# Last-use pools, earlier fetches and a kept-clear last chain in a two-layer graph kernel

## The chip, the core and the metric

The kernel runs as one program on one core of a Trainium2 chip. A core has five engines with a queue of instructions each, worked off strictly in order: PE (matrix products into eight banks of PSUM), DVE and ACT (elementwise work), POOL (here it only issues gathers) and SP (here it only issues transfers). Engines wait for each other and for transfers through semaphores; whatever stands behind a waiting instruction in its queue waits too. The metric is the device time of one execution in microseconds (us), the median of several runs.

## The reference

Two rounds of a graph network over 6250 nodes and 100000 edges, then a residual and a layer norm:

```python
def _gin_agg(h, src, dst, eps, n_nodes):
    agg = jax.ops.segment_sum(h[src], dst, num_segments=n_nodes)
    return (1.0 + eps) * h + agg

h = _gin_agg(x, src, dst, eps1, n)            # width 256
h = relu(h @ W1a + b1a)
h = relu(h @ W1b + b1b)                       # width 512; the kernel calls it h1
h = _gin_agg(h, src, dst, eps2, n)            # width 512
h = relu(h @ W2a + b2a)
out = h @ W2b + b2b                           # width 256
x = _layernorm(x + out, axis=-1)
```

The edges are sorted by `dst`, and `dst` is the square of a uniform number, so low nodes receive most of the edges.

## The kernel before, in words

Nodes are held in 49 tiles of 128 rows (tile 48 has 106). Edges are held in 782 chunks of 128. The kernel works in two layers, one after the other, and each layer sums messages in two ways.

*Heavy tiles (0 to 6)* receive so many edges that their sums are a dense product: a table of counts (how many edges run from each source to each node) times the rows. In layer 1 the counts are built on the core ("counting"), used (L1606) and also stored in DRAM (`counts`). In layer 2 they come back as `ci`, are converted by ACT into `cf` (L1399), and multiply the rows of h1, which are fetched as `xr` for a *range* of four tiles at a time and split by ACT and DVE into an upper and a lower half (L1362, L1363, L1367). There are 13 ranges; range 12 holds tile 48 alone, range 11 tiles 44 to 47. The products of one range with one heavy tile are eight matmuls, upper and lower half in turn (L1470, `second_products`). `AHEAD2` ranges, from the highest down, are already worked in layer 1, once counting is over.

*All other edges* are gathered: POOL issues one indirect DMA per chunk (L488), 494 in each layer, into two rings (`early`, and in layer 2 also `late`). The rings hold six pieces of four chunks. PE adds up a piece with a one-hot matrix `sel` (L1066), ACT copies the sum out of PSUM (`split`, L1100 or L1108), PE puts the parts of a group of chunks in their places (L1119, with `to`), and DVE adds them to the tiles' accumulators (L1129). Groups are worked from the highest nodes down to the lowest.

When a tile has all its sums, its *dense* part follows: PE transposes the accumulator (L1165), ACT copies it (`zt`, L1177), PE multiplies by the first weights (L1204), ACT applies bias and relu (`ht`, L1214), PE multiplies by the second weights (L1233). Then DVE and ACT finish h1 (`h1r`, L1243 and L1245) and ACT stores it (L1246) in layer 1; in layer 2 residual and norm follow, and SP stores the output. An accumulator is seeded: SP fetches the tile's own rows, and ACT scales them by 1 + eps (L916).

The last group of layer 1 reaches tiles 6 and 7. So layer 2 begins with a group (`FORE`, 12 chunks) that gathers only from rows which do not include tiles 6 and 7 (`h1[: GAP + 1]`); what comes from these two is counted and added separately (`late_edges`, `adding_late`). All later gathers of layer 2 may touch any row of h1, so they wait until tiles 6 and 7 are stored.

The order of instructions on every engine is written by a planner, `Plan`, while the program is built. It plays the kernel through with costs that stand in the code (`LOAD = 6.0`, `COUNTS = 12.0`, `SEEDS = (6.0, 12.0)`, `PASS`, `act()`, `dve()`), and each step asks for an engine with a priority (a smaller number goes first). The planner is run for each layer apart. It decides orders alone; when something runs is left to the semaphores.

On-chip memory comes from stacked pools. Those of layer 1 are closed before those of layer 2 are opened in the same place, so a tile of layer 2 waits until the tile that lay there in layer 1 has been used for the last time:

```python
for name in ("first", "keep1", "loan1")        # layer 1
for name in ("keep2", "loan2")                 # layer 2
acc_room = Tiles(keep if once else loan, [P, TILES, width], F32, "acc", ACCS if once else ACCS2)
```

`first` holds layer 1's weights, `keep1` everything from `sel` to `h1r` and the accumulators. The pool `wide2` on the other side, for the second products, is opened when counting is over.

Of the kernel before, what the change touches and what calls it, by code (L numbers as in the profile page):

```python
# [10 lines left out]
F32 = mybir.dt.float32  # L11
# [35 lines left out]
PASS = 0.00042  # L47
LATE = (6, 8)
HASTE = -14.0
AHEAD2 = 1  # L50
ACCS2 = 4
AFTER = 4.0
# [300 lines left out]
def tile_gin_residual_layernorm(  # L353
# [105 lines left out]
    FORE = next(g for g in range(BEGIN[1], NG) if lo[g] >= max(HEAVY[1], LATE[0]))  # L459
    orders = {1: list(reversed(range(BEGIN[0], NG)))}  # L460
    orders[2] = [FORE] + [g for g in reversed(range(BEGIN[1], NG)) if g != FORE]
# [7 lines left out]
    FORE0, FOREN = groups[FORE][0], len(members[FORE])  # L469
# [7 lines left out]
    def gather(number, i, table, width, *places):  # L477
# [7 lines left out]
        if number == 2 and pieces[number][i][0] == FORE:  # L485
            table, rows_in, first = h1[: GAP + 1, :], fore, FORE0
# [281 lines left out]
    def ordered(ctx):  # L768
# [17 lines left out]

        def layer(number, pools, table, width, scale, weights, ba, wide, at=None, aside=None, right=None):
# [5 lines left out]
            keep, loan, last_ = pools  # L793
# [14 lines left out]
            def reach(g):  # L808

                return range(lo[g] if once or SAME else max(lo[g], tiles), hi[g] + 1)  # L810

            last_use, uses = {}, {t: 0 for t in range(NT)}
            for k, g in enumerate(order):
                for t in reach(g):
                    last_use[t] = k
                    uses[t] += 1
            heavy = range(tiles)
            blocks, taken = [], None
            for t in reversed(range(NT)):
                single = last_use.get(t, -1) >= len(order) - ENDING  # L820
                if taken and not single and len(taken) < TILES and (t >= tiles or (tiles - 1 - t) % TILES):
                    taken.insert(0, t)
                else:
                    taken = [t]
                    blocks.append(taken)
                    if single:
                        taken = None
# [22 lines left out]
            def fetch_rows(i):  # L850
                nonlocal pool_free
                if i < len(pieces[number]):
# [5 lines left out]
                    plan.at(pool_free + LANDINGS[number - 1], arrived[i].set)  # L858

# [4 lines left out]
                keep, [P, 2, width], F32 if once else F32R, "split", SPLITS if once else 3  # L864
# [5 lines left out]
            acc_room = Tiles(  # L870
                keep if once else loan, [P, TILES, width], F32, "acc", ACCS if once else ACCS2
            )
            if not once:
                r_room = Tiles(loan, [P, TILES, D], F32, "r", 2)
                mv_room = Tiles(loan, [P, TILES, 2], F32, "mv", 2)
                st_room = Tiles(loan, [P, 6], F32, "st", 3)
                sd_room = Tiles(loan, [P, TILES], F32, "sd", 2)
                rs_room = Tiles(loan, [P, TILES], F32, "rs", 2)

            if not once:  # L880
                apart = loan.tile([P, len(reach(FORE)), width], F32, name="apart")
                assert all(len(blocks[block_of[t]]) == 1 for t in reach(FORE))

            def seeding(bs, want):
                for i, b in enumerate(bs):
# [5 lines left out]
                    if not once and ts[0] in reach(FORE):  # L891
                        token = Place()
                        token.tile = apart[:, ts[0] - lo[FORE] :]
                    else:
                        token = yield ("get", acc_room, 0)
                    a = token.tile
                    where = natural if once else place
# [1324 lines left out]
```

## Time and profile before

| | us |
|---|---|
| median of 3 runs (lowest, highest) | 1317.04 (1312.97, 1320.39) |
| the profiled execution | 1315.43 |
| its span, first to last instruction | 1313.6 |
| PE busy / POOL busy / DVE busy / ACT busy | 1183.7 / 955.4 / 874.6 / 619.8 |
| DMA | 306.27 MB, mean 233 GB/s |
| mean granted TensorE clock | 0.960 of full |

The page's second part, the span in 40 slices of 32.8 us (each digit is a busy share in tenths), shows the change of layers in the slices that begin at 624 and 657 us:

```profile
PE   6869889999898899779859998999899999999986
...
POOL 6777777777777777777567777777777777777760
PEclk9879999999999999987879999999999999999999
...
GB/s 217 149 131 207 203 210 223 183 202 214 204 201 215 223 197 156 172 227 169 257 293 321 326 252 324 238 301 277 301 254 309 292 308 311 281 234 237 240 229 39
```

POOL shows 7 or so because the part of a gather that counts as busy is 0.95 us of every 1.25 us. In rows of the timeline below, a row gives the start, the length, the engine, the source line and operation, the tiles written and read, how many instructions were merged (`x8`), and in brackets how long the engine had been idle and what ended that. A planned matmul over f32 data shows up as two rows of MATMUL.

### The profile page before, as it was taken

How to read it: one execution, taken by the hardware profiler on the slowest of the kernel's cores; microseconds unless marked ns; L12 is line 12 of the kernel's file. 1: busy time of each engine (PE TensorE's matmuls, PEld its weight loads, DVE VectorE, ACT ScalarE, POOL GpSimd, SP SyncE). 2: the span in 40 equal slices, each digit the busy share in tenths (PEclk: the TensorE clock that was granted, in tenths of full speed). 3: DMA queues.
4: the chain of work that ended last, by engine and by line, in shares of the span. 5: the costliest groups of instructions: out<-in, count | busy, mean ns of one | idle time of the engine just before them, and what ended most of it. 6: DMA issues, size and time to landing. Idle time of an engine off the chain costs nothing.

```text
span 1313.6 us, 18937 instructions
## 1 busy us (share of the span) xinstructions
PE 1183.7 (90%) x6117; PEld 760.0 (58%) x6117; DVE 874.6 (67%) x2070; ACT 619.8 (47%) x1137; POOL 955.4 (73%) x1001
## 2 busy tenths in 40 slices
PE   6869889999898899779859998999899999999986
PEld 4435455555554455345426676777677667677666
DVE  7978986877886776653147877777666665563343
ACT  6217777575657652464254444344244444242212
POOL 6777777777777777777567777777777777777760
PEclk9879999999999999987879999999999999999999
DMA  6446677666667765575889989788889899877771
GB/s 217 149 131 207 203 210 223 183 202 214 204 201 215 223 197 156 172 227 169 257 293 321 326 252 324 238 301 277 301 254 309 292 308 311 281 234 237 240 229 39
DMA packets 161072, 306.27 MB, mean 233 GB/s; under 512 B 25625, under 2 KB 93103, under 8 KB 160964
## 3 DMA queue, kind: packets, MB, share of 16 engines
q0 software_dynamic: 63232, 194.31, 48.0%
q1 hardware_dynamic: 76778, 86.19, 19.9%
q10 hardware_dynamic: 20954, 24.45, 5.2%
q8 instruction: 52, 0.85, 0.3%
q14 instruction: 56, 0.46, 0.1%
HBM read 274.42 MB, written 30.44 MB: 232 GB/s over the span
## 4 chain that ended last, share of the span: by engine, by line
PE 46%; DMA 16%; DVE 12%; POOL 10%; issue 8%; ACT 6%; ACTq 1%; DVEq 1%; SPq 0%; POOLq 0%
PE bank L1204 12%; POOL early L488 9%; PE bank L1233 9%; PE bank L1066 8%; PE bank L1470 8%; DMA early<-in_x_dram,srcs 5%; PE bank L1119 3%; DMA early<-h,places 3%; PE bank L1606 3%; DVE acc L1129 3%; DVE at L1897 2%; DMA late<-h,places 2%; DMA sown<-h 2%; PE bank L1165 2%; PE bank L1712 1%
## 5 line engine op out<-in xcount | busy, mean ns | idle before, releaser
L488 POOL DMA_INDIRECT early<-in_x_dram,srcs x494 | 480.9, 973 | 153.8 <-issue 128.8
L488 POOL DMA_INDIRECT late<-h,places x242 | 232.6, 961 | 79.6 <-issue 60.3
L488 POOL DMA_INDIRECT early<-h,places x240 | 228.6, 952 | 73.1 <-issue 59.7
L1129 DVE SCALAR_TENSOR_TENSOR acc<-bank,mask,acc 128x256 f32<-128x256 f32 (+1 forms) x360 | 206.6, 606 | 65.0 <-PE bank L1119 58.3
L1233 PE MATMUL bank<-w1b_s,ht 128*128 128x512 f32 (+1 forms) x392 | 184.5, 595 | 2.0 <-ACT ht L1214 1.4
L1204 PE MATMUL bank<-zt,w2a_s 128*128 128x256 f32 (+2 forms) x896 | 181.7, 356 | 3.6 <-ACT zt L1177 2.4
L1066 PE MATMUL bank<-early,sel 128*32 128x256 f32 (+1 forms) x1492 | 139.6, 485 | 40.2 <-DMA early<-in_x_dram,srcs 24.4
L1204 PEld LDWEIGHTS bank<-zt,w2a_s 128*128 128x128 f32 x896 | 154.2, 192 | 33.3 <-issue 8.4
L1470 PE MATMUL bank<-upper,cf 128*128 128x512 f32 (+1 forms) x343 | 148.4, 433 | 0.0
L1470 PE MATMUL bank<-xr,cf 128*128 128x512 f32 (+1 forms) x343 | 136.5, 398 | 0.0
L1897 DVE TENSOR_TENSOR at<-bank,at 128x490 f32 x174 | 116.0, 667 | 25.5 <-ACT cf L1555 13.7
L940 DVE TENSOR_TENSOR sel<-iota,slot 128x256 f32<-128x256 f32 (+3 forms) x116 | 50.9, 439 | 106.0 <-PE bank L1066 98.8
L1119 PE MATMUL bank<-split,to 128*128 128x256 f32 (+2 forms) x340 | 105.7, 430 | 10.4 <-ACT split L1100 4.1
L1214 ACT ACTIVATE ht<-bank,b2a_s 128x256 f32<-128x256 f32 (+2 forms) x112 | 44.6, 443 | 147.9 <-PE bank L1204 144.8
L1066 PEld LDWEIGHTS bank<-early,sel 128*32 128x32 f32 x1492 | 39.5, 113 | 127.6 <-issue 85.3
L1233 PEld LDWEIGHTS bank<-w1b_s,ht 128*128 128x128 f32 (+1 forms) x392 | 72.7, 189 | 67.8 <-issue 54.1
L1606 PE MATMUL bank<-xh,cf 128*128 128x512 f32 (+1 forms) x343 | 100.6, 429 | 11.6 <-DVE xh L1534 10.3
L1399 ACT CAST cf<-ci 128x512 fp32r<-128x512 uint16 (+1 forms) x91 | 54.1, 595 | 116.9 <-PE bank L1470 95.0
L1204 PE MATMUL bank<-zt,w1a_s 128*128 128x256 f32 (+2 forms) x432 | 102.4, 386 | 5.4 <-ACT zt L1177 1.7
L1712 PE MATMUL bank<-cb,ca 128*128 128x490 f16 x288 | 89.0, 386 | 14.3 <-DVE at L1897 5.3
L1680 DVE TENSOR_SCALAR cb<-numbers,spot 128x490 f16<-128x490 f16 x288 | 91.2, 358 | 15.7 <-PE bank L1712 15.5
L1233 PE MATMUL bank<-w2b_s,ht 128*128 128x256 f32 (+1 forms) x392 | 100.0, 386 | 0.0
(176 smaller groups left out, 1692.2 us busy)
## 6 DMA issues: line engine op xcount, KB each, us to landing
raw<-in_x_dram SPq DMA_DIRECT2D x48, 512.0 KB
h<-h1r ACTq DMA_DIRECT2D x48, 256.0 KB
xr<-h SPq DMA_DIRECT2D x11, 1024.0 KB
counts<-ci ACTq DMA_DIRECT2D x84, 128.0 KB
ci<-counts SPq DMA_DIRECT2D x84, 128.0 KB
acc<-h SPq DMA_DIRECT2D x18, 512.0 KB
early<-in_x_dram,srcs POOLq DMA_INDIRECT x494
acc<-in_x_dram SPq DMA_DIRECT2D x21, 256.0 KB
```

Source lines behind the costliest of these rows:

```text
L488: nc.gpsimd.indirect_dma_start(out=rows_[:, j, :], out_offset=None, in_=table, in_offset=bass.IndirectOffsetOnAxis(ap=rows_in[:, c - first ...
L1066: mm = nc.tensor.matmul(pm[b * SLOTS : (b + 1) * SLOTS], sel[:, c - groups[g][0], :], rows_[:, l, :], start=(c == part[0]), stop=(c == par ...
L1119: nc.tensor.matmul(pu[:, i * width : (i + 1) * width], to[:used], split[:used, l, :], start=(once or l == 0), stop=(once or l == 1),)
L1129: nc.vector.scalar_tensor_tensor(acc[t], pu[:, i * width : (i + 1) * width], mask[:, t - lo[g], g : g + 1], acc[t], op0=ALU.mult, op1=ALU.add,
L1204: nc.tensor.matmul(ph[:, (f - o) * TILES * P : (f - o) * TILES * P + nb], wa[:, k, f * P : (f + 1) * P], zt[:, k, :nb], start=(k == 0), st ...
L1233: nc.tensor.matmul(po[:m], ht[:, f, i * P : i * P + m], wb[:, f, :], start=(f == 0), stop=(f == KH - 1),)
L1399: nc.scalar.copy(cf_token.tile[:, :n, :].rearrange("p k j -> p (k j)"), token.tile[:, : n * P],)
L1470: nc.tensor.matmul(bank[token.number][:, :width], cf[:m, j, :], of[:m, j, :], start=(j == 0 and of is upper), stop=(j == len(ks) - 1 and o ...
L1606: nc.tensor.matmul(bank[tokens[i].number][:, : 2 * width], cf[:m, j, :], xh[:m, j, :, :].rearrange("p a d -> p (a d)"), start=(k == 0), st ...
L1680: made = nc.vector.tensor_scalar(token.tile, numbers, spot[:, c : c + 1], None, op0=ALU.is_equal)
L1712: mm = nc.tensor.matmul(bank[token.number][:, : NT * W], a.tile[:, c % BATCH, :], b.tile, start=(j == 0), stop=(j == n - 1),)
L1897: nc.vector.tensor_tensor(to, bank[token[0].number][:, : NT * W].rearrange("p (k w) -> p k w", w=W), to, op=ALU.add,)
```

## The change

The change has five parts, all of them in the order and the places of work; the gathers and their order on POOL stay as they are.

1. *Pools.* Both layers' pools are stacked by the time of last use: `leave` (what is used to the end: h1r, the norm's tiles, layer 2's weights), `hold` (split, zt, ht, acc), `keep` (sel, to, cf, late, sown), and above them layer 1's `loan1`. So `keep2` lies where tiles were that layer 1 is done with first.
2. *Fetched when counting is over.* `AHEAD2` goes from 1 to 2: besides range 12, range 11 is fetched and multiplied in layer 1. A new step, `first_seeds`, fetches four accumulators' seeds for layer 2 (tiles 42 to 48) and has ACT scale them; their four buffers lie in `wide2`, which gives up one `ci` buffer (6 to 5).
3. *The last chain.* From 1.5 us (`LEAD`) before the planned landing of layer 1's last gather until the planner has placed the last dense matmul (`settled`), none of the second products' and seeds' steps may be placed (`busy`).
4. *Layer 2's beginning.* Its weights are fetched 5 us after its planned start (`SOWN2`) and no longer as its first transfer; the planner starts `late_rows` apart from `late_edges`.
5. *The late edges' counts* are computed with the one-hot rows as the wide operand: 12 matmuls of 256 columns and two transposes, for 24 of 32 columns.

The diff, cut to its core:

```diff
+SOWN2 = 5.0
+LEAD = 1.5
-AHEAD2 = 1
+AHEAD2 = 2
+SOW = 8.0
...
+            quiet, settled, finished = [], Event(plan), []
+
+            def busy():
+                return once and quiet and plan.now >= quiet[0] and not settled.done
...
+                    if once and i == len(pieces[number]) - 1:
+                        quiet.append(pool_free + LANDINGS[number - 1] - LEAD)
...
-            zt_room = Tiles(keep, [P, kk, TILES * P], F32, "zt", 2)
-            ht_room = Tiles(keep, [P, KH, TILES * P], F32, "ht", 2)
+            zt_room = Tiles(hold, [P, kk, TILES * P], F32, "zt", 2)
+            ht_room = Tiles(hold, [P, KH, TILES * P], F32, "ht", 2)
             if once:
-                h_room = Tiles(keep, [P, H], F32, "h1r", 3)
+                h_room = Tiles(leave, [P, H], F32, "h1r", 3)
...
+            def first_seeds():
+                yield ("rest", SOW)
...
+                for ts in some[:ACCS2]:
+                    for t in ts:
+                        yield ("until", stored[t])
+                    a = begun_with["pool"].tile(
+                        [P, TILES, H], F32, tag="acc2", name="acc2", bufs=ACCS2
+                    )
+                    in_rows(ts, a, h1, place)
...
+                    todo.append((ts, a))
+                yield ("rest", SEEDS[1])
+                for ts, a in todo:
+                    if busy():
+                        yield ("until", settled)
+                    yield ("on", "ACT", act(len(ts) * H), 6)
+                    nc.scalar.activation(
+                        a[:, : len(ts), :], a[:, : len(ts), :], AF.Copy, scale=e1[:, 1:2]
+                    )
+                    begun_with["seeds"].append((ts, a))
...
+                    finished.append(t)
+                    if len(finished) == NT:
+                        plan.then(settled.set)
...
-                ci_room = Tiles(pool2, [P, RANGE * P], mybir.dt.uint16, "ci2", 6)
+                ci_room = Tiles(pool2, [P, RANGE * P], mybir.dt.uint16, "ci2", 5)
...
+                            if busy():
+                                yield ("until", settled)
                             token = yield ("get", banks, first or 3)
                             yield ("on", "PE", 2 * PASS * len(ks) * width, first or 3)
...
                     second_products(list(reversed(range(len(ranges))))[:AHEAD2])
+                    plan.start(first_seeds())
...
-                yield ("rest", WEIGHTS)
+                yield ("rest", WEIGHTS if once else SOWN2 - plan.now)
...
-                for name in ("first", "keep1", "loan1")
+                for name in ("first", "leave1", "hold1", "keep1", "loan1")
...
-                inner.enter_context(tc.tile_pool(name=name, bufs=1)) for name in ("keep2", "loan2")
+                for name in ("leave2", "hold2", "keep2")
```

How the orders move is shown at three places. The first is SP's queue where layer 1 has just stored its last counts, and ACT's queue shortly after. Lines of the changed kernel are higher: its L1388 and L1393 are L1307 and L1312 of before, L1470 is L1387 (`ci`), L966 scales the new seeds, L1255 is L1177 (`zt`). SP before (the weights that follow `ci_5837` are layer 2's first transfers):

```order
L1387 DMA ci_5780<-counts 128x128
L1387 DMA ci_5782<-counts 128x128
L1312 DMA raw<-in_x_dram 106x256
L1387 DMA ci_5837<-counts 128x128
L735 DMA w2a_s<-in_L_gnn_W2a_dram 128x4x512
L736 DMA w2b_s<-in_L_gnn_W2b_dram 128x4x256
L737 DMA b2b_s<-in_L_gnn_b2b_dram 128x256
L1307 DMA xr<-h_60 128x4x512
```

and now (`acc_5804` to `acc_5812` are the four seeds):

```order
L1470 DMA ci_5786<-counts 128x128
L1388 DMA acc_5804<-h_60 128x512
L1393 DMA acc_5804<-h_60 106x512
L959 DMA acc_5804<-h_60 22x512
L1388 DMA acc_5808<-h_60 128x2x512
L1388 DMA acc_5810<-h_60 128x2x512
L1388 DMA acc_5812<-h_60 128x2x512
L1393 DMA raw<-in_x_dram 106x256
L1388 DMA xr<-h_60 128x4x512
L1470 DMA ci_5853<-counts 128x128
L1470 DMA ci_5857<-counts 128x128
L1470 DMA ci_5868<-counts 128x512
```

The seeds and range 11's rows now stand ahead of the sixth and seventh `ci` of range 12. ACT at the place that uses them, before:

```order
L1532 COPY bank_96<-raw 106x256
L1399 CAST cf<-ci_5782 128x128
L1399 CAST cf<-ci_5837 128x128
L1177 COPY zt<-bank_100 128x2x128
L1412 COPY whole_acc<-bank_94 128x512
L1245 ACTIVATE h1r<-h1r 128x512
L1246 DMA h_60<-h1r 128x512
```

and now:

```order
L1619 COPY bank_96<-raw 106x256
L1484 CAST cf<-ci_5853 128x128
L966 ACTIVATE acc_5804<-acc_5804,e_81 128x1024
L1445 CAST upper<-xr 128x512
L1446 COPY bank_100<-xr 128x512
L1484 CAST cf<-ci_5857 128x128
L966 ACTIVATE acc_5808<-acc_5808,e_81 128x1024
L1255 COPY zt<-bank_97 128x2x128
L1326 ACTIVATE h1r<-h1r 128x512
```

Two seeds' scalings and the first copies of range 11 now stand between the sixth `cf` and the copy `zt` of a dense part.

The second place is PE at layer 1's last gathers: the last pieces' sums (`early,sel`), tile 8's dense part (the w1b row or rows next to the sums), the last group's placing (`split,to`), and the dense parts of tiles 6 and 7. Before:

```order
L1066 MATMUL bank_101<-early,sel 32x256 x4
L1233 MATMUL bank_100<-w1b_s,ht 128x512 x4
L1066 MATMUL bank_101<-early,sel 32x256 x8
L1119 MATMUL bank_96<-split,to 128x256
L1165 MATMUL bank_95<-ident,acc 128x128 x2
L1165 MATMUL bank_97<-ident,acc 128x128 x2
L1204 MATMUL bank_98<-zt,w1a_s 128x128 x4
```

and now:

```order
L1557 MATMUL bank_96<-upper,cf 128x512
L1557 MATMUL bank_96<-xr,cf 128x512
L1144 MATMUL bank_98<-early,sel 32x256 x4
L1311 MATMUL bank_101<-w1b_s,ht 128x512 x2
L1197 MATMUL bank_95<-split,to 128x256
L1311 MATMUL bank_101<-w1b_s,ht 128x512 x2
L1243 MATMUL bank_99<-ident,acc 128x128 x2
L1243 MATMUL bank_94<-ident,acc 128x128 x2
L1282 MATMUL bank_97<-zt,w1a_s 128x128 x4
```

Four of range 11's seven products (the two rows at the top end the fourth) now stand ahead of the last sum, the other three behind tile 6's and 7's dense parts; and tile 8's second weights, which stood ahead of the last pieces' sums, now stand behind them, around the placing.

The third place is PE at the end of the program, from the sum of the last piece. Before:

```order
L1066 MATMUL bank_95<-late,sel 32x512 x4
L1204 MATMUL bank_101<-zt,w2a_s 128x128 x8
L1119 MATMUL bank_100<-split,to 128x512 x2
L1204 MATMUL bank_99<-zt,w2a_s 128x128 x8
L1233 MATMUL bank_97<-w2b_s,ht 128x256 x2
L1204 MATMUL bank_96<-zt,w2a_s 128x128 x8
L1233 MATMUL bank_97<-w2b_s,ht 128x256 x2
L1233 MATMUL bank_98<-w2b_s,ht 128x256 x4
L1165 MATMUL bank_94<-ident,whole_acc 128x128 x4
L1204 MATMUL bank_95<-zt,w2a_s 128x128 x8
L1165 MATMUL bank_101<-ident,apart 128x128 x4
L1204 MATMUL bank_100<-zt,w2a_s 128x128 x8
```

and now (from here to its end):

```order
L1144 MATMUL bank_95<-late,sel 32x512 x4
L1197 MATMUL bank_96<-split,to 128x512 x2
L1243 MATMUL bank_101<-ident,whole_acc 128x128 x4
L1243 MATMUL bank_98<-ident,apart 128x128 x4
L1282 MATMUL bank_100<-zt,w2a_s 128x128 x8
L1282 MATMUL bank_97<-zt,w2a_s 128x128 x8
L1282 MATMUL bank_94<-zt,w2a_s 128x128 x8
L1282 MATMUL bank_99<-zt,w2a_s 128x128 x8
L1311 MATMUL bank_95<-w2b_s,ht 128x256 x2
```

The dense parts of two tiles that stood behind the last sum now stand ahead of it; only those of tiles 6 and 7 follow it.

More of the change, by code (lines that the diff above doesn't have):

```diff
@@ L785, in ordered, with layout, reach @@
         begun_with = {}
+        def layout(number):
+            tiles, order = HEAVY[number - 1], orders[number]
+            def reach(g):
+                return range(lo[g] if number == 1 or SAME else max(lo[g], tiles), hi[g] + 1)
+            last_use, uses = {}, {t: 0 for t in range(NT)}
+            for k, g in enumerate(order):
+                for t in reach(g):
+                    last_use[t] = k
+                    uses[t] += 1
+            blocks, taken = [], None
+            for t in reversed(range(NT)):
+                single = last_use.get(t, -1) >= len(order) - ENDING
+                if taken and not single and len(taken) < TILES and (t >= tiles or (tiles - 1 - t) % TILES):
+                    taken.insert(0, t)
+                else:
+                    taken = [t]
+                    blocks.append(taken)
+                    if single:
+                        taken = None
+            return reach, uses, blocks
         def layer(number, pools, table, width, scale, weights, ba, wide, at=None, aside=None, right=None):
@@ L806, in __init__ @@
                     self.make = lambda: pool.tile(shape, dtype, tag=name, name=name, bufs=bufs)
[L808 to L816, printed above, removed]
-            heavy = range(tiles)
[L818 to L827, printed above, removed]
+            reach, uses, blocks = layout(number)
+            heavy = range(tiles)
             block_of = {t: b for b, ts in enumerate(blocks) for t in ts}
@@ L890, in seeding @@
                         yield ("until", want[b])
-                    if not once and ts[0] in reach(FORE):
+                    if not once and ts[0] in FORETOLD:
                         token = Place()
-                        token.tile = apart[:, ts[0] - lo[FORE] :]
+                        token.tile = apart[:, ts[0] - FORETOLD[0] :]
                     else:
@@ L896, in seeding @@
                     a = token.tile
+                    if not once and begun_with["seeds"] and begun_with["seeds"][0][0] == ts:
+                        begun_with["seeds"].pop(0)
+                        held[b] = token
+                        for i, t in enumerate(ts):
+                            acc[t] = a[:, i, :]
+                            ready[t].set()
+                        settle(ts[0])
+                        continue
                     where = natural if once else place
@@ L1032, in adding_late @@
                     )
-                for token in tokens:
-                    token.release()
+                counts_token.release()
+                sown["late"].used()
                 plan.then(plan.start, then)
@@ L1944, in ordered @@
         with ExitStack() as inner:
-            pool = [
+            first, leave, hold, keep, loan = (
                 inner.enter_context(tc.tile_pool(name=name, bufs=1))
-                for name in ("first", "keep1", "loan1")
-            ]
-            w1a_s, w1b_s, fetch = first_two(pool[0], False)
+                for name in ("first", "leave1", "hold1", "keep1", "loan1")
+            )
+            w1a_s, w1b_s, fetch = first_two(first, False)
             nonlocal near
-            near = pool[0].tile([P, NC], F32, name="near")
+            near = first.tile([P, NC], F32, name="near")
             right = ExitStack()
@@ L1958, in ordered @@
             layer(
-                1, (*pool[1:], last_), x, D, e1[:, 0:1], (w1a_s, w1b_s, b1b_s, fetch), b1a_s, H, at,
+                1, (keep, loan, last_, hold, leave), x, D, e1[:, 0:1], (w1a_s, w1b_s, b1b_s, fetch), b1a_s, H, at,
                 aside, right,
```

142 lines of the change are left out of this document (91 added, 51 removed).

## The prediction

> **What bounds the kernel now.** I read the waits of POOL first, because its instructions are the same in both kernels and in the same order.
>
> ```profile
> POOL early L488 <- issue: 191.0, 627, 0.3
> ...
> POOL early L488 <- DMA acc<-h: 11.0, 1, 11.0
> ...
> POOL late L488 <- DMA h<-h1r: 6.2, 1, 6.2
> ```
>
> A row tells who waited, for what, the total in us, how often, and the longest wait. Apart from 0.3 us of issue before each gather, POOL waits twice for long, and both waits lie at the change of layers. Its timeline there:
>
> ```profile
> 635.32 0.95 POOL L488 DMA_INDIRECT early<-in_x_dram,srcs  x1 [0.30 <-issue]
> 636.57 0.95 POOL L488 DMA_INDIRECT early<-in_x_dram,srcs  x1 [0.30 <-issue]
> ...
> 648.55 0.95 POOL L488 DMA_INDIRECT early<-h,fore  x1 [11.04 <-DMA acc<-h]
> ...
> 662.31 0.95 POOL L488 DMA_INDIRECT early<-h,fore  x1 [0.30 <-issue]
> 669.48 1.01 POOL L488 DMA_INDIRECT late<-h,places  x1 [6.22 <-DMA h<-h1r]
> ...
> 1276.26 0.95 POOL L488 DMA_INDIRECT late<-h,places  x1 [0.30 <-issue]
> ```
>
> So the kernel is a chain of gathers 1.25 us apart, a change of layers from 636.57 to 669.48, again gathers without a pause until 1276.26, and a tail of 37.3 us. An edit shows in the time only if it moves 669.48 (everything behind moves along) or shortens the tail. Which instruction ends the two waits is told by ACT's stores of h1:
>
> ```profile
> 640.56 0.33 ACTq L1246 DMA_DIRECT2D h<-h1r  x1
> ...
> 662.52 0.33 ACTq L1246 DMA_DIRECT2D h<-h1r  x1
> ```
>
> The first is tile 8's, 8.0 us ahead of 648.55; the label `acc<-h` names another transfer, but gathers of rows without tiles 6 and 7 must wait for tile 8. The second is the last tile's, 7.0 us ahead of 669.48. In between lie 12 gathers, 15.0 us.
>
> PE is the second bound. By stretches (length, then busy time of PE, PEld, DVE, ACT, POOL, granted clock, DMA share, GB/s):
>
> ```profile
> 640.00:660.00 20.00, 14.91 (x60) 9.57 (x61) 1.46 (x3) 4.15 (x12) 8.70 (x10) 0.74 1.00 326
> ...
> 850.00:900.00 50.00, 50.00 (x269) 37.13 (x268) 39.21 (x77) 21.56 (x41) 37.95 (x40) 1.00 0.89 295
> ```
>
> Inside layer 2 PE has no gap, but it keeps pace with POOL. At the change of layers the DMA engines are full, 326 GB/s.
>
> **The change part by part.** *The range moved into layer 1.* Range 11 is seven products; a product is eight matmuls, and 24 of them take 5.70 us, so 1.9 us each and 13.3 us in all:
>
> ```profile
> 682.62 5.70 PE bank L1470 x24
> ```
>
> They leave layer 2, where PE is full, but POOL does not wait there, so this shortens nothing until the tail. Four of them (7.6 us) now stand ahead of layer 1's last sum, in a stretch where PE has this to do:
>
> ```profile
> 620.56 1.05 PE L1204 MATMUL bank<-zt,w1a_s 128*128 128x128 f32 x8
> ...
> 635.44 3.70 PE L1233 MATMUL bank<-w1b_s,ht 128*128 128x512 f32 x8
> 639.07 0.64 PE L1066 MATMUL bank<-early,sel 128*32 128x256 f32 x8
> 643.97 1.08 PE L1066 MATMUL bank<-early,sel 128*32 128x256 f32 x8 [4.26 <-DMA early<-in_x_dram,srcs]
> ```
>
> Before, PE ran dry at 639.7, waited 4.3 us for the last gather, and ended the last sum at 645.05. Now, from 620.56: the same 19.15 us to 639.7, less tile 8's 3.7 (it stands behind the sum), plus 7.6, plus 0.64 for the last sum, 23.7 us: T = 644.3, if nothing else waits. The wait for the gather has been filled.
>
> *The fetches.* SP and ACT around the new fetches:
>
> ```profile
> 600.62 2.74 SPq L1387 DMA_DIRECT2D ci<-counts  x6
> ...
> 615.20 0.30 ACT L1399 CAST cf<-ci 128x128 fp32r<-128x128 uint16 x1
> 616.62 0.30 ACT L1399 CAST cf<-ci 128x128 fp32r<-128x128 uint16 x1 [1.13 <-PE bank L1606]
> 618.56 0.37 ACT L1177 COPY zt<-bank 128x256 f32<-128x256 f32 x1 [1.64 <-PE bank L1165]
> ...
> 662.97 3.23 ACT L916 ACTIVATE acc<-acc,e 128x1024 f32<-128x1024 f32 x3 [0.48 <-ACT h1r L1245]
> ```
>
> After five `ci` (602.9) SP now issues the four seeds (2048 KB), the 106-row piece of x, range 11 (1024 KB) and only then the sixth and seventh `ci`: 3.3 MB. Gathers of 131 KB each 1.25 us take 105 GB/s of the 326, which leaves 221: 15.0 us; had they all 326, 10.2. A transfer's fixed part I bound by a 128 KB gather, 4.19 us from issue to landing, 0.95 of it on POOL and 0.4 of it the bytes, so 2.8:
>
> ```profile
> 587.50 4.19 DMA early<-in_x_dram,srcs
> ```
>
> The sixth `ci` lands at 620.7 (bound: 615.9), and ACT, which converted it at 615.20, waits for it with everything behind. Behind it stand two `cf` (0.3 each), two seeds (1.08 each) and two copies (1.2), 3.9 us, and then the `zt` that tile 0's dense part needs: 624.6 for 618.56. PE follows 0.7 us later, at 625.3 for 620.56: a wait of 4.7 us that delays all of PE's queue, the last sum too. The bound gives 620.5, no wait. I take the 4.7, since the gathers do not pause: T = 649.0 for 645.05.
>
> *The last chain.* Behind T stand 3.7 us of tile 8's second weights and 0.45 of placing. Before, its store came 1.4 us after those (639.1 to 640.56); now two `zt` copies of 0.4 are ahead of it on ACT: T + 6.3. From store to gather it took 8.0 and 7.0 us while the DMA was full. What filled it, layer 2's weights, range 11 and the seeds, has been moved away, so I take 4.3, near the uncrowded 4.19. Tile 8's rows are there at T + 10.6, 12 gathers more, and POOL's long run begins at T + 25.6; before it was T + 24.4. Tiles 6 and 7 begin 1.8 us later behind T (the filled-in matmuls) but run at full clock, 1.5 us saved of 20; they are stored before that, so the first gathers decide. POOL: 674.6, that is +5.1 (with the bound: 669.9, +0.4).
>
> *Pools.* They end a wait of DVE, which could not write layer 2's first `sel`:
>
> ```profile
> 668.90 0.56 DVE L940 TENSOR_TENSOR sel<-iota,slot 128x384 f32<-128x384 f32 x1 [7.08 <-DMA h<-h1r]
> ```
>
> These 7.1 us lay beside gathers that PE needed later, and POOL does not wait for them: nothing, at most the 7.1 on PE. *Weights later:* 1.7 MB, first used at 721.60 (below), about 50 us behind the fetch; nothing, or at 221 GB/s 7.7 us if that cover were gone. The late edges' counts are some 3 us of PE and DVE beside POOL's run: nothing.
>
> ```profile
> 721.60 3.40 PE L1204 MATMUL bank<-zt,w2a_s 128*128 128x234 f32 x16 [1.17 <-ACT bank L1363]
> ```
>
> *The tail.* From the last piece's sum:
>
> ```profile
> 1281.41 1.07 PE L1066 MATMUL bank<-late,sel 128*32 128x512 f32 x8
> 1282.41 2.05 PE L1204 MATMUL bank<-zt,w2a_s 128*128 128x128 f32 x16
> 1284.22 0.71 PE L1119 MATMUL bank<-split,to 128*128 128x512 f32 x2
> ...
> 1291.79 0.60 PE L1165 MATMUL bank<-ident,whole_acc 128*128 128x128 f32 x4
> ...
> 1301.67 2.76 PE L1233 MATMUL bank<-w2b_s,ht 128*128 128x256 f32 x12
> ```
>
> Tiles 6 and 7 take 12.6 us from their first transpose to PE's end. That transpose comes 9.4 us after the sum, because two other tiles' dense parts are in the queue. Now these are ahead of the sum. What must come in between is shown by an earlier sum that ended at 1262.07:
>
> ```profile
> 1262.13 0.58 ACT L1108 CAST split<-bank 128x512 fp32r<-128x512 f32 x1 [2.45 <-PE bank L1066]
> ...
> 1262.74 0.69 DVE L1110 TENSOR_TENSOR split<-bank,split 128x512 fp32r<-128x512 f32 x1 [3.84 <-ACT split L1108]
> ...
> 1284.97 0.75 DVE L1129 SCALAR_TENSOR_TENSOR whole_acc<-bank,mask,whole_acc 128x512 f32<-128x512 f32 x1 [1.11 <-PE bank L1119]
> ```
>
> 1.4 us, 0.75 for placing and 0.85 for the add: 3.0. Gain 6.4, provided that PE has worked off the other tiles before the last landing; the 13.3 us taken out of layer 2 pay for that. But PE then idles for over 2 us of that chain, and this is what idling cost:
>
> ```profile
> 1142.66 1.07 PE L1066 MATMUL bank<-late,sel 128*32 128x512 f32 x8 [2.00 <-DMA late<-h,places]
> ```
>
> and the stretch behind it:
>
> ```profile
> 1144.00:1147.40 3.40, 3.40 (x10) 2.63 (x9) 1.87 (x5) 0.53 (x2) 2.65 (x3) 0.50 0.83 258
> ```
>
> After 2.00 us of idling the clock was 0.50 for 3.4 us, so 1.7 us were lost. I take one such stretch: the tail gains 4.7. The Trainium skill ("TensorE: Matmul & The Clock Gate", Part 1) says that the clock falls to half after an idle window of about 3.4 us. By it the shorter pauses of this tail would cost nothing, and the sum would be 1.7 us lower; the row at 1142.66 speaks against it, unless the windows lay badly.
>
> **Sum.** +5.1 at the change of layers and -4.7 in the tail, +0.4: 1315.8 against the profiled execution's 1315.43. The median of the runs is 1317.04, 1.6 above that execution: 1317.4.
>
> **The rivals.** *Faster:* the fetches land by 616 and PE's order fits. Then T is bound by the last landing, 636.57 + 4.6, plus the sum, 641.8; POOL starts at 667.4 (-2.1), and the tail gains its whole 6.4: -8.5, 1308.5. For it speaks that PE's idle 4.3 us and the full DMA behind 634 are both removed; against it, that PE's 23.7 us from 620.56 end at 644.3 even without a wait.
>
> *Slower:* ACT's queue at the sixth `ci` holds PE much longer. With the DMA at the 180 GB/s that are left beside what 600 to 636 already carries (326 less 146, below), the fetch takes 18.4 us, `zt` comes at 628.0 and the wait is 8.1; a pause like that halves the clock as the 2.00 did, two stretches, 3.4. T = 655.8, POOL 681.4, +11.9; less the tail's 4.7 is +7.2, 1324.2. It decides from a wait of PE of about 8 us.
>
> ```profile
> 600.00:636.00 36.00, 34.69 (x175) 20.26 (x174) 9.61 (x19) 17.23 (x41) 27.17 (x30) 0.89 0.51 146
> ```
>
> *The tail stays:* PE is not ahead at the end, because its gaps move with the gathers. Then +5.1 alone, 1322.1. PE without a gap at 850 speaks for it.
>
> **How the numbers follow.** The forecast has 0.42, faster 0.23, slower 0.25, the unshortened tail 0.10. Half a percent, 6.6 us, is about what a measurement of this kernel can tell from no change; the forecast and the last rival lie within it: same 0.52, faster 0.23, slower 0.25. The forecast's own range is 1311 (no wait of PE at 620, whole tail) to 1322. The range over the cases is 1306 to 1328.
>
> **What would show it.** Right: PE waits near 620 for ACT's `zt`, which waits for a transfer; the last sum of layer 1 ends near 649; tile 8's store, not the last one, starts the long run, POOL's second wait being 0.3; the run begins near 675; and the first transpose of tile 6 follows the last sum by some 3 us. Wrong: any long wait of POOL inside layer 2, which the old profile has nowhere, or a last sum ahead of 643.

## The result and the profile after

The changed kernel takes 1331.50 us (median of 8, 1324.89 to 1337.35) against 1318.51 us (median of 8): ratio 1.0102, 95% interval 1.0075 to 1.013. It is slower, by twice what a measurement can tell from no change, and lies 3.5 us outside the predicted range. The span of its profiled execution is 1328.7 us for 1313.6, so 15.1 us are to be found.

POOL's rows after the change, from its timeline: the last gather of layer 1, the first of layer 2, the first of the long run, a wait that the old profile has nowhere, and the last gather.

```profile
639.18 0.94 POOL L494 DMA_INDIRECT early<-in_x_dram,srcs  x1 [0.30 <-issue]
...
664.71 0.95 POOL L494 DMA_INDIRECT early<-h,fore  x1 [24.59 <-PE bank L1282]
...
680.20 1.43 POOL L494 DMA_INDIRECT late<-h,places  x1 [0.30 <-ACT bank L1446]
...
726.96 1.36 POOL L494 DMA_INDIRECT early<-h,places  x1 [3.81 <-PE bank L1144]
...
1292.62 0.95 POOL L494 DMA_INDIRECT late<-h,places  x1 [0.30 <-issue]
```

Set beside the rows of before:

| | before | after | later by |
|---|---|---|---|
| last gather of layer 1 | 636.57 | 639.18 | 2.6 |
| end of layer 1's last sum | 645.05 | 655.29 | 10.2 |
| long run begins | 669.48 | 680.20 | 10.7 |
| last gather | 1276.26 | 1292.62 | 16.4 |
| end of the span | 1313.6 | 1328.7 | 15.1 |

So 10.7 us are lost by the beginning of the long run, 5.6 inside it, and the tail gives 1.2 back.

**The change of layers.** ACT's and PE's timelines, at the place where the last sum is made late:

```profile
623.59 0.41 ACT L1612 CAST xh<-raw 106x256 fp32r<-106x256 f32 x1 [10.98 <-DMA raw<-in_x_dram]
...
627.50 0.30 ACT L1484 CAST cf<-ci 128x128 fp32r<-128x128 uint16 x1 [3.22 <-DMA ci<-counts]
...
631.03 0.35 ACT L1255 COPY zt<-bank 128x256 f32<-128x256 f32 x1
```

```profile
624.78 0.79 PE L1694 MATMUL bank<-xh,cf 106*128 106x512 f32 x1 [8.65 <-DVE xh L1621]
625.37 3.19 PE L1311 MATMUL bank<-w1b_s,ht 128*128 128x512 f32 x4
629.10 1.88 PE L1311 MATMUL bank<-w1b_s,ht 128*128 128x512 f32 x4
631.43 1.16 PE L1282 MATMUL bank<-zt,w1a_s 128*128 128x128 f32 x8 [0.45 <-ACT zt L1255]
...
654.65 0.64 PE L1144 MATMUL bank<-early,sel 128*32 128x256 f32 x8
```

ACT stands still for 10.98 us on the last piece of x, 106 KB, which DVE and PE need for layer 1's own products; PE's long wait, 8.65 us for `xh`, is for the same piece. SP issued that piece behind 2 MB of seeds for layer 2. Then ACT waits 3.22 us more for the sixth `ci`, issued behind a further 1 MB. Tile 0's `zt` comes at 631.03 for 618.56. After its pause PE does the same four matmuls in 3.19 us that otherwise take 1.88. SP's issues, and the stretches (length, busy PE, PEld, DVE, ACT, POOL, granted clock, DMA share, GB/s):

```profile
607.14 1.47 SPq L1393 DMA_DIRECT2D raw<-in_x_dram  x1
608.66 6.94 SPq L1388 DMA_DIRECT2D xr<-h  x1
...
682.56 0.43 SPq L741 DMA_DIRECT2D w2a_s<-in_L_gnn_W2a_dram  x1
...
685.38 2.94 SPq L1388 DMA_DIRECT2D xr<-h  x1
```

```profile
603.90:624.00 20.10, 10.59 (x64) 6.28 (x63) 2.52 (x4) 7.62 (x19) 15.22 (x17) 0.85 0.93 290
...
620.00:624.00 4.00, 0.00 (x0) 0.00 (x0) 0.00 (x0) 0.41 (x2) 2.92 (x4) 0.50 0.98 306
624.00:628.00 4.00, 3.22 (x5) 1.57 (x6) 2.07 (x5) 0.78 (x3) 3.08 (x4) 0.50 0.45 139
```

SP's queue did not run evenly. Its transfers carried 1.91 MB from 604 to 613, but 0.20 MB from 613 to 616 and 0.11 MB from 624 to 627, where ACT waits for the `ci`. SP was held up in the issue of range 11's rows from 608.66 to 615.60, and issued the sixth `ci` only at 615.70. What held the queue in these pauses stays open.

**Layer 2's opening.** The weights, issued from 682.56 on, stand ahead of the second range's rows (`xr`, 685.38). ACT, PE and POOL wait for these in turn; POOL's part is the 3.81 us at 726.96 above:

```profile
708.15 0.62 ACT L1445 CAST upper<-xr 128x512 fp32r<-128x512 f32 x1 [13.69 <-DMA xr<-h]
```

```profile
711.37 1.52 PE L1197 MATMUL bank<-split,to 128*128 128x512 f32 x2 [10.62 <-ACT split L1186]
```

**The tail**, all engines:

```profile
1299.60 1.06 PE L1144 MATMUL bank<-late,sel 128*32 128x512 f32 x8
...
1302.14 0.29 ACT L1354 ACTIVATE sd<-mv,lneps 128x1 f32<-128x1 f32 x1 [2.21 <-DVE mv L1339]
1302.34 0.57 ACT L1186 CAST split<-bank 128x512 fp32r<-128x512 f32 x1
...
1305.29 1.11 PE L1243 MATMUL bank<-ident,whole_acc 128*128 128x128 f32 x4 [0.84 <-DVE whole_acc L1207]
```

The two other tiles' dense parts are ahead of the last sum, as planned. But PE was still busy with them when the rows had landed: the sum begins 6.98 us behind the last gather for 5.15. Then ACT's copy of the sum stands behind `sd`, a step of another tile's norm that waits for DVE. From sum to transpose it is 4.63 us, for 9.31 before and 3.0 forecast.

### The profile page after: what moved, and what is told of

Its sections match the earlier page's. It is cut to its first block, busy times and chain, and to the rows that moved or that the text cites. A ratio compares the mean times of both kernels' runs of the same rounds, so it can differ in the third digit from the quotient of the medians.

```text
span 1328.7 us, 18925 instructions
## 1 busy us (share of the span) xinstructions
PE 1185.3 (89%) x6107; PEld 761.7 (57%) x6107; DVE 878.2 (66%) x2070; ACT 619.4 (47%) x1138; POOL 960.4 (72%) x1001
## 4 chain that ended last, share of the span: by engine, by line
PE 47%; DMA 13%; DVE 12%; POOL 10%; issue 7%; ACT 7%; SPq 1%; ACTq 1%; DVEq 1%; POOLq 0%
PE bank L1282 14%; PE bank L1311 9%; POOL early L494 8%; PE bank L1144 8%; PE bank L1557 8%; DMA late<-h,places 4%; DMA early<-in_x_dram,srcs 3%; PE bank L1197 3%; PE bank L1694 3%; DVE at L1985 2%; POOL late L494 2%; PE bank L1800 2%; DVE acc L1207 2%; DMA xr<-h 2%; PE bank L1243 2%
## 5 line engine op out<-in xcount | busy, mean ns | idle before, releaser
L1282 PE MATMUL bank<-zt,w2a_s 128*128 128x256 f32 (+2 forms) x896 | 184.5, 361 | 2.4 <-ACT zt L1255 2.4
L1282 PE MATMUL bank<-zt,w1a_s 128*128 128x256 f32 (+2 forms) x432 | 98.7, 374 | 5.2 <-ACT zt L1255 2.5
L1800 PE MATMUL bank<-cb,ca 128*128 128x490 f16 x288 | 89.6, 388 | 13.5 <-DVE at L1985 5.6
L1502 DVE TENSOR_TENSOR whole_acc<-bank,whole_acc 128x512 f32<-128x512 f32 x84 | 57.4, 686 | 64.8 <-PE bank L1557 64.8
```

Of the source, the lines that this page charges most:

```text
L1282: nc.tensor.matmul(ph[:, (f - o) * TILES * P : (f - o) * TILES * P + nb], wa[:, k, f * P : (f + 1) * P], zt[:, k, :nb], start=(k == 0), st ...
L1502: nc.vector.tensor_tensor(sums_of[t], bank[token.number][:, :width], sums_of[t], op=ALU.add)
L1800: mm = nc.tensor.matmul(bank[token.number][:, : NT * W], a.tile[:, c % BATCH, :], b.tile, start=(j == 0), stop=(j == n - 1),)
```

## The experiments

Three theories: **A**, the order of SP's fetches holds ACT, and with it PE, at the change of layers; **B**, what counts there is PE's own work, the range 11 products ahead of the last sum; **C**, the weights hold the second range's rows in layer 2 (its rival **D**: PE is behind there for other reasons). All ratios are to the kernel before, run on the same chip. "Last sum" and "long run" count from the start of layer 1's last gather to the end of its last sum and to the beginning of POOL's long run. This takes out when that last gather came, 636.2 to 641.6 in these kernels. A row's stretches come from one trace, the ratios from 7 to 12 executions.

| kernel | ratio (95%) | last sum | long run | its length | tail |
|---|---|---|---|---|---|
| before | 1 | 8.5 | 32.9 | 606.8 | 37.3 |
| the change | 1.0102 (1.0075 to 1.013) | 16.1 | 41.0 | 612.4 | 36.1 |
| e1 seeds behind | 1.0024 (1.0006 to 1.0042) | 11.9 | 34.4 | 613.2 | 31.3 |
| e2 seeds in layer 2 | 1.0034 (1.0017 to 1.0051) | 7.5 | 31.0 | 621.9 | 30.5 |
| e3 one range | 1.0020 (1.0002 to 1.0037) | 12.7 | 34.8 | 609.1 | 35.2 |
| e4 weights behind | 1.0068 (1.0049 to 1.0086) | 17.3 | 42.2 | 608.6 | 35.7 |
| e5 seeds and weights behind | 0.9959 (0.9937 to 0.9981) | 13.5 | 35.1 | 611.4 | 32.5 |
| e5b, the same again | 0.9974 (0.9958 to 0.9990) | 9.2 | 30.9 | 609.7 | 30.9 |
| e6 = e2, weights behind | 0.9988 (0.9966 to 1.0010) | 8.9 | 32.4 | 611.1 | 30.6 |
| e7 = e3, both behind | **0.9945** (0.9927 to 0.9964) | 3.9 | 27.4 | 606.9 | 35.6 |
| e8 one range, seeds in layer 2, weights behind | **0.9951** (0.9934 to 0.9969) | 3.6 | 26.2 | 608.5 | 36.9 |
| e9b before, weights behind | 1.0029 (1.0008 to 1.0049) | 9.3 | 31.0 | 611.1 | 38.1 |
| e10b not kept clear | 1.0058 (1.0039 to 1.0077) | 17.3 | 41.8 | 614.2 | 30.1 |
| e11b another order | 1.0067 (1.0043 to 1.0092) | 22.2 | 43.9 | 616.2 | 31.0 |
| e12b range 11 behind the chain | 0.9972 (0.9957 to 0.9988) | 4.0 | 33.9 | 607.7 | 30.7 |

e5 and e5b are one program with the same order on every engine. Their traces differ by 4.3 us in the last sum, 4.2 in the beginning of the long run, 1.7 in its length and 1.6 in the tail, so a smaller difference between two rows shows nothing by itself. For e5b 12 to 14 and 34 to 36 us were forecast, and 9.2 and 30.9 came.

e9, e10, e11, e12 and a repeat of e7 also ran on two chips on which the kernel before took 1628 and 1605 us and POOL's gathers paused about every 12 us in layer 1 and every 18 in layer 2. The ratios there were 0.9973, 1.0198, 1.0047, 1.0115 and 0.9900. With such pauses they are not set beside the others, and e9 to e12 were run again (the labels with b); e10's and e12's ratios there are higher by over 1%.

**e1 to e4: one part undone at a time.**

```diff
-SOW = 8.0          # e1: the seeds are issued behind the piece of x, six ci and range 11's rows
+SOW = 20.0
-                    plan.start(first_seeds())            # e2: the seeds in layer 2, as before
+                    begun_with["seeds"] = []
-AHEAD2 = 2         # e3: range 11 in layer 2, as before
+AHEAD2 = 1
-SOWN2 = 5.0        # e4: xr of the second range ahead of the weights; every other queue the same
+SOWN2 = 10.0
```

> Theory A (the order of the fetches): in the changed kernel ACT waits 10.98 us at 612.6 for the 106-row piece of x, which SP issues behind four seeds of 2 MB, and PE's queue waits with it. Here the seeds are issued behind that piece, the seventh ci and four ci of range 11. ACT's wait for the piece is gone, PE's wait there falls from 8.65 us to under 3, the last sum of layer 1 ends near 647 for 655.3, POOL's long run begins near 671 for 680.2 and the time falls by about 9 us, to 1322. Theory B (PE's own work: four products of range 11 now stand ahead of the last sum): the waits may move, but the last sum ends within 2 us of 655.3 and the time stays at 1330.

> The seeds are fetched at the beginning of layer 2 again, as before the change; range 11 stays in layer 1. Theory A: the piece of x is again the next issue behind five ci, ACT does not wait for it, the last sum ends near 646 and the long run begins near 671. What the seeds cost now is a later start of DVE's adds in layer 2, which POOL does not see: about 1322. Theory B: the products of range 11 are as many as in the changed kernel, the last sum stays within 2 us of 655.3 and the time at 1330.

> Only range 12 is worked in layer 1, the seeds stay where the change puts them. Theory A: the 106-row piece still stands behind 2 MB of seeds, so ACT's wait for it stays at 8 to 11 us; PE has 7.6 us less to do ahead of the last sum, which ends near 649 to 652; the long run begins near 675, and the time is 1325 to 1328. Theory B: with range 11 gone the last sum ends near 645 as before the change, the long run begins by 670 and the time is 1320 or less.

> One exchange on SP's queue and nothing else: the rows of layer 2's second range (xr) are issued ahead of the 1.7 MB of weights, not behind them. Theory C (the weights hold up xr: ACT waits 13.69 us for it at 694.5, PE 10.6 us behind it, and at 726.96 POOL waits 3.81 us because a ring is still full): ACT's wait shrinks to 5 us or less, POOL has no wait above 0.5 us behind the start of its long run, the last gather comes 3.8 to 5.6 us earlier, and the time falls by about 4.5 us, to 1327. Rival D (PE is late in layer 2 because layer 1 ended late, whatever ACT waits for): POOL's wait near 727 stays, and the time is 1331.

ACT's cast of the 106-row piece in e1 and in e3:

```profile
618.83 0.43 ACT L1612 CAST xh<-raw 106x256 fp32r<-106x256 f32 x1
```

```profile
621.90 0.41 ACT L1612 CAST xh<-raw 106x256 fp32r<-106x256 f32 x1 [8.92 <-DMA raw<-in_x_dram]
```

With the seeds behind it, the piece is there before ACT asks; with the seeds ahead ACT waits 8.92 us, whether range 11 is there (10.98) or not. A's mechanism holds: in e1 and e2, where ACT's wait is gone, the long run begins 6.6 and 10.0 us sooner than in the change, and the ratio falls by 0.7 to 0.8% (in part by the tail, which is 4.8 and 5.6 us shorter in their orders). But B is not dead. e1, without that wait, has its last sum 11.9 us behind the last gather, not the forecast 6 (its end was at 652.8, not 647). And e3, in which ACT still waits, missed A's 1325 to 1328: its ratio is as low as e1's, 1.0020 or about 1321, near B's 1320, and its long run begins 6.2 us sooner. Nor does e3 part A from B: with range 11 its 1 MB left SP's queue ahead of the sixth `ci`, and ACT's second wait, 3.22 us, is gone too. e2 gains most at the change of layers and gives it back: POOL waits 3.39, 6.30 and 5.69 us in its long run.

e4 settles C against D, since it changes SP's queue alone. ACT's wait for `xr` falls from 13.69 us to this,

```profile
ACT upper L1445 <- DMA xr<-h: 4.2, 1, 4.2
```

POOL's wait near 727 is gone, and the long run lasts 608.6 us for 612.4: 3.8 of the 5.6 us. The rest lies in gathers that themselves took longer, as the 1.43 us at 680.20, in e4 too. In the ratios e4 gains 0.34%, 4.5 us, with intervals that overlap a little.

**e5 to e8: the parts together.** e5 has `SOW = 20.0` and `SOWN2 = 20.0`; e6 e2's line and `SOWN2 = 20.0`; e7 `AHEAD2 = 1`, `SOW = 20.0`, `SOWN2 = 10.0`; e8 `AHEAD2 = 1`, e2's line, `SOWN2 = 10.0`.

> Seeds issued behind the piece of x, the ci and range 11's rows (as in the run with the seeds behind, ratio 1.0024), and layer 2's weights behind its second range's rows. Theory A+C (two fetches, each in front of what another engine waits for): the two gains add up. POOL's waits of 4.80 and 1.38 us at 722.7 and 739.2 go, the long run lasts near 607 us for 613.2, and the ratio to the kernel before falls from 1.0024 to about 0.998. Rival D (PE is behind in layer 2 because of what it has to do): the long run still lasts 611 us or more, the ratio stays at 1.002.

> Range 11 in layer 1, no early seeds, weights behind the second range's rows. With the seeds back in layer 2 POOL waited 3.39, 6.30 and 5.69 us in its long run (621.9 us). If the weights caused this (theory C) the long run falls to about 609 us, and the ratio from 1.0034 to about 0.994: its change of layers took only 31.0 us from the last gather of layer 1 to the long run (32.9 before the change) and its tail 30.5 (37.3 before). If the late seeds caused it (ACT waited 12.21 us for the first of them at 661.8), the long run stays above 617 us and the ratio at 1.002 or more.

> Only range 12 in layer 1, the early seeds behind the piece of x and both ci, the weights behind the second range's rows and two ci. Theory A: against the run with one range (ACT waited 8.9 us for the piece, last sum at 648.9, long run from 671.0, ratio 1.002) ACT's wait goes, the last sum ends at 643 to 646, the long run begins at 666 to 668 and the ratio falls to about 0.998. Theory B (only PE's own work counts at the change of layers): the long run begins at 671 again, ratio 1.002.

> Neither range 11 nor the seeds are fetched in layer 1, the weights come behind the second range's rows: what is left of the change are the pools, the late edges' counts and the chain kept clear. If the loss of the change lay in the fetches alone, this is the kernel before or a little better: the long run begins at 664 to 669, the tail is 35 to 37 us as with one range, ratio 0.996 to 1.000. If the pools or the chain kept clear cost something themselves, the ratio is above 1.002.

e7 and e8 beat the kernel before by half a percent, more than was expected of e7 (0.998). They lie within each other's intervals: fetching the seeds in layer 1 is worth nothing that can be measured. e5 met its ratio, but not its long run: 611.4 us, as rival D had it, with a wait of POOL of 5.42 us at 737.5 (in e5b no such wait is left). e6 lies between its two forecasts, and 3.20 and 2.16 us of waits stayed. The rows of e7's PE and POOL timelines show the change of layers as it can be:

```profile
639.45 1.07 PE L1144 MATMUL bank<-early,sel 128*32 128x256 f32 x16
```

```profile
636.66 0.95 POOL L494 DMA_INDIRECT early<-in_x_dram,srcs  x1 [0.30 <-issue]
643.78 0.94 POOL L494 DMA_INDIRECT early<-h,fore  x1 [6.17 <-PE bank L1243]
...
664.06 1.03 POOL L494 DMA_INDIRECT late<-h,places  x1 [5.60 <-DMA ci<-counts]
```

The last sum ends at 640.5, 3.9 us behind the last gather, tile 8's store (640.94) releases POOL in 2.8 us for 8.0 before, and the last store decides the long run. The 9 us around the last landing, of the kernel before and of e7:

```profile
636.00:645.00 9.00, 4.74 (x24) 1.50 (x22) 0.69 (x1) 0.63 (x1) 1.21 (x2) 0.85 1.01 325
```

```profile
636.00:645.00 9.00, 7.17 (x34) 3.42 (x35) 1.57 (x3) 2.03 (x6) 2.25 (x3) 0.89 0.20 67
```

The DMA carries 67 GB/s there instead of 325 (103 in e8).

**e9b: is it the weights alone?** In the kernel before, layer 2's weights are fetched 10 us after its planned start instead of at once; on SP they stand right behind the second range's rows.

> The kernel before, with layer 2's weights issued behind its second range's rows, and no other part of the change. If moving the 1.7 MB of weights out of layer 1's last chain is what the kernels with the fetches put right gain (theory W), the last sum ends 3 to 5 us behind the last gather of layer 1 for 8.5, the stores of h1 take about 3 us to release POOL for 8.0 and 7.0, the long run begins 26 to 28 us behind the last gather for 32.9, and the ratio is 0.994 to 0.997. If it is the pools (theory P), the long run begins 31 us or more behind the last gather and the ratio is 0.999 or more.

No: 1.0029, and the long run begins 31.0 us behind the last gather, as theory P had it. The weights left the stretch and the seeds moved up into it:

```profile
637.59 0.32 SPq L1307 DMA_DIRECT2D acc<-h  x1
```

against 646.99 before. The stretch from 636 to 645 still carried 233 GB/s, the last rows were waited for until 648.19, and POOL waited 3.13 us at 731.9. In e8 the same seeds, in the new pool, go out at 617.4; SP has no wait there like the 16.7 us for PE's second products (L1470) that end at 637.59 in e9b. So the weights moved behind do not gain alone. That it is the pair, with pools that let the seeds go out 20 us ahead of the last chain, is argued: e8 differs from e9b also in the late edges' counts and the chain kept clear, and the pools alone were not tried.

**e10b and e11b: the chain kept clear, and the order.** e10b lets `busy()` return False; e11b has `SOW = 8.5`, which leaves SP's fetches there in their order and has all of layer 2 ordered afresh.

> The changed kernel, but the second products and the seeds may be placed in layer 1's last chain (busy is never true); the fetches are the same. If the chain kept clear earns something, tiles 6 and 7 are stored later, POOL waits a second time (over 2 us) before its long run, which begins over 43 us behind the last gather of layer 1 (41.0 in the changed kernel), and the ratio is 1.012 or more. If it earns nothing, the ratio is 1.007 to 1.012.

> The changed kernel with the seeds' step 0.5 us later in the planner: SP's fetches at the change of layers in the same order, one seed fewer scaled by ACT ahead of tile 0's zt, all of layer 2 ordered afresh. Theory A: ACT still waits 9 to 12 us for the piece of x and the long run begins 39 to 42 us behind the last gather (41.0 in the changed kernel). If the planner's order decides how much of the tail is gained, the tail is 31 to 33 us for 36.1, and the ratio 1.005 to 1.008; if PE's lateness decides, it stays at 35 to 37, ratio 1.009 or more.

Without the clear chain POOL's second wait is 1.36 us for 0.30, and the long run begins 0.8 us later, far less than e5 and e5b differ: that the guard earns anything is not shown. The ratio came out below both expectations, with a tail of 30.1 us. e11b has A's stall (11.6 us), POOL waits of 5.81 and 3.15 us in the long run, and a tail of 31.0, as forecast if the order decides. Its long run begins later than forecast; one more product and tile 8's second weights stand ahead of its last sum. Only the change and e4, whose orders differ in SP's queue alone, have tails near 36 among the nine kernels with range 11 in layer 1. e4 has no stall of POOL in layer 2, so that is not the reason. The tail of e10b, for the rows of the change above:

```profile
1301.58 1.06 PE L1144 MATMUL bank<-late,sel 128*32 128x512 f32 x8 [1.25 <-DMA late<-h,places]
...
1302.70 0.59 ACT L1186 CAST split<-bank 128x512 fp32r<-128x512 f32 x1 [2.58 <-PE bank L1144]
...
1306.17 0.65 PE L1243 MATMUL bank<-ident,whole_acc 128*128 128x128 f32 x4 [1.60 <-DVE whole_acc L1207]
```

PE waits for the rows (the sum begins 4.06 us behind the last gather), ACT copies at once, and the transpose follows 3.5 us after the sum.

**e12b: B by itself.** e5's lines and `LEAD = 12.0` for 1.5: range 11's products stand behind tile 6's and 7's dense part.

> Both fetches behind, and range 11's products behind the last chain (kept clear from 12 us ahead of the last landing). Theory B in addition to A: the last sum ends 4 to 6 us behind the last gather of layer 1 for 13.5 with the products ahead of it, the long run begins 27 to 30 us behind it for 35.1, the tail stays at 31 to 33 us, and the ratio is near 0.990. If the products ahead of the sum cost nothing, the long run begins 34 us or more behind the last gather and the ratio stays at 0.996. A third way: the products run late in layer 2's opening, POOL waits there for PE (over 3 us in all), and the ratio is 0.993 or more in spite of an early long run.

> Both fetches behind, range 11's products ahead of the last sum: the comparison for the run with the products behind the chain. Ratio 0.996 as before, within 0.002; the last sum 12 to 14 us behind the last gather, the long run 34 to 36 us.

B holds for the last sum, beside A: it comes 4.0 us behind the last gather, against 9.2 (e5b) and 13.5 (e5). But the time is the same, 0.9972 and 0.9974, not B's 0.990. The third way came: POOL's second wait grew to 12 us:

```profile
672.48 0.94 POOL L494 DMA_INDIRECT late<-h,places  x1 [11.99 <-ACT cf L1484]
```

```profile
671.34 0.40 PE L1557 MATMUL bank<-xr,cf 128*128 128x512 f32 x1
```

The last store of h1 was issued at 659.99; from there to the gather it took 7.0 us in the kernel before and 6.7 in e7, here 12.5. POOL started 0.7 us behind PE's last product of range 11. The pool with `late` lies over layer 1's `loan1`, which holds the `cf` that these products read. That this overlap is the reason is argued from the code and the 0.7 us; no run took it away.

## Why the prediction was wrong

*The spine.* Right, as far as it went: apart from the issue time POOL's long waits are at the change of layers, and an edit shows only there, in the long run or in the tail. "POOL does not wait" inside layer 2 was taken over from the old profile; the change broke it.

*The fetches: the step that failed first.* "The sixth `ci` lands at 620.7" rested on 221 GB/s left beside the gathers. Measured were 290 GB/s in all from 603.9 to 624, 185 beside the gathers' 105, close to the slower rival's 180. And the step priced the `ci` but not the piece of x, though it named it in SP's row; ACT met that one first, at 623.6, and the `ci` at 627.5. PE's long wait was for the piece (8.65 us); the wait for `zt` that was forecast is 0.45 us. Nor was it a matter of bandwidth alone: the 185 is the mean of a queue that stood nearly still twice, and the last 3 us of ACT's waiting fall into the second pause. From there the working holds: `zt` 631.0 for 624.6, 6.4 late; T 655.3 for 649.0, 6.3 late. The last sum came in at the slower rival's 655.8, with a PE wait of 8.65 us for its 8.1. That it fits to half a microsecond is partly luck: the rival took 3.4 us for the clock, where four matmuls lost 1.3 (3.19 for 1.88), and its wait was for the `ci`. The full clock that the forecast took for granted was lost there: 0.50 for some 3 us behind the pause. The Trainium skill ("DMA: Bandwidth & Descriptors", section "Queues, rings and completion order") says that a queue's descriptors are taken in order on each DMA engine, which agrees with a small piece landing 15 us behind its issue at the end of 2 MB, and with no wait in e1.

*The last chain.* Right: T + 5.5 for tile 8's store (6.3 taken), 3.9 us to the gather (4.3), the first gathers decide (second wait 0.30), long run at T + 24.9 (25.6). Forecast +5.1, measured +10.7. That the last gather came 2.6 us later is no part of it: PE had no pause between 640.5 and T, so its own lateness set T.

*Weights later: "nothing".* Wrong: the long run lost 5.6 us. The cover of the weights' own use was priced, not what stands behind them on SP's queue. The second range's rows do, ACT's queue stands behind these, and a ring of POOL behind PE. e4 returns 3.8 of it; the gathers that took longer were in no sum.

*Pools.* Right as far as the change itself goes: no gain by them shows in it, though no run has them alone. What they seem to make possible, seeds at 617 (e8), the change spent on issuing these ahead of layer 1's own piece.

*The tail: -4.7, measured -1.2.* The size failed, in the proviso that PE "has worked off the other tiles": +1.8. The 3.0 us from sum to transpose were 4.63, for ACT's `sd` was not in the sum: ACT's copy began 1.68 us behind it. (Before it was 9.31, where 9.4 was read.) The one half-clock stretch is there: tiles 6 and 7 take 14.39 us for 12.64, +1.75, where 1.7 was taken. The mechanism was right: with range 11 in layer 1, the seven kernels of another order have tails of 30.1 to 32.5 us, 4.8 to 7.2 below before.

*Sum.* 5.6 + 5.6 + 3.5 us of misses make the 14.7 between +0.4 and +15.1. The slower rival had the place and the size at the change of layers (+11.9, measured +10.7), but not the stall in layer 2. Its chance, 0.25, was too low: the piece of x stood in the difference of the orders and was not followed into ACT's queue.

## What to carry to other kernels

A fetch moved forward on an in-order queue delays everything that stands behind it there, so price it by what the first consumer behind it holds up, not by its own use: 2 MB that nothing needed before layer 2 held the long run back by some 7 to 10 us (e1, e2). Follow each overtaken transfer into the queue of the engine that takes it, and from there to the engine that waits for that one. When a planner writes the order, a small change of one cost reorders everything behind it. Compare stretch by stretch from a common event (here: from the last gather), and the tail apart. Take two traces of one program before a difference of a few us is read; here they were 4 us apart.

## What the runs showed of the hardware

Pauses shorter than 3 us halved PE's clock in one tail and not in another. In these traces the granted clock changes only at steps of 3.41 us, and whether it falls goes with how busy PE was in the whole step ahead. A step of the change's tail, with the pause of 2.30 us in it, and the step behind:

```profile
1300.44:1303.86 3.42, 0.84 (x6) 0.31 (x2) 2.68 (x8) 0.77 (x2) 0.00 (x0) 1.00 0.11 38
1303.86:1307.27 3.41, 2.57 (x10) 1.79 (x10) 1.41 (x2) 0.59 (x1) 0.00 (x0) 0.50 0.37 115
```

the steps around the 2.00 us at 1142.66 of the kernel before:

```profile
1140.59:1144.01 3.42, 1.42 (x14) 0.50 (x11) 0.23 (x1) 0.23 (x1) 2.64 (x3) 1.00 1.04 383
1144.01:1147.42 3.41, 3.41 (x10) 2.64 (x9) 1.88 (x5) 0.54 (x2) 2.67 (x3) 0.50 0.82 256
```

and in e10b, with pauses up to 1.60 us:

```profile
1302.56:1305.97 3.41, 1.88 (x10) 1.05 (x6) 2.54 (x6) 0.88 (x2) 0.00 (x0) 1.00 0.00 0
1305.97:1309.38 3.41, 2.68 (x22) 2.45 (x23) 1.29 (x4) 1.18 (x2) 0.00 (x0) 1.00 0.25 77
```

Over the traces of the 15 rows of the table, no step with PE busy for less than 1.4 us kept the full clock for the next one, and none with more than 2.3 us lost it; between the two both happened. The Trainium skill ("TensorE: Matmul & The Clock Gate", Part 1) asks for an idle window of about 3.4 us. The 8.65 us pause at the change of layers agrees; the tail of the change does not, unless a window that is only mostly idle counts, as these rows suggest.

An issue can itself take long: SP needed 6.94 us for the one transfer at 608.66, where 0.37 to 0.43 is usual, and everything behind it on SP waited.

One thing stays open. Layer 1's last gather came 2.6 us later in the change, 4.3 in e1 and 0.3 earlier in e3, although these kernels have the same order of instructions up to about 600 us; most of the difference arises between 425 and 520 us. e5 and e5b, one program, differ by 1.4 us in the same gather.
